# Two expert layers by seven products of quarters, with the layernorm split in two

## The chip, the cores and the metric

The kernel runs on one core of a Trainium2 chip. The metric is device time in microseconds for one execution, and each version is timed several times; the median is what counts. All data and all matmuls of the part in question are f32.

## The reference

A graph of 6250 nodes with 256 features each passes a graph convolution and then a mixture of experts. Cut to what matters:

```python
x = x + gnn(layernorm(x), edges)          # x@W, normalised neighbour sums, bias, PReLU
xf = layernorm(x)                          # (6250, 256)
# one routing decision for the whole batch, from the mean token: top 2 of 8 experts
h = gelu(einsum('nd,edf->enf', xf, W1) + b1)      # 256 -> 512, exact gelu
y = einsum('enf,efd->end', h, W2) + b2            # 512 -> 256
o = sum over the two experts of w[e] * y[e]
x = x + (layernorm(o + xf) * gamma + beta)
```

The mean token decides the two experts and their weights, so that every node goes through the same two experts. The change is only in `h`, `y` and the last layernorm.

## The kernel before, in words

The nodes lie in 49 tiles of 128 rows (the last has 106). The first 785 us or so are the graph convolution, the routing and the load of the two experts' weights. W2 and b2 are scaled by the experts' weights as they arrive (L1337), so that the two experts can be summed in one PSUM accumulation.

The expert stage (L1344 on) works on groups of four tiles, `TN = 4`: group 0 is one tile, groups 1 to 11 are whole, group 12 holds the short last tile. The order of every engine's work is the order in which it is written (`manual_schedule`), so each engine takes its instructions in line, and an instruction that waits holds all behind it on that engine. The steps of a group are:

- `take` (L998): SyncE loads the four tiles `xt` from HBM.
- `turn` (L1003): VectorE normalises each tile, `yt = (xt - mean) * rstd` (L1010); TensorE transposes it into PSUM (L1015); ScalarE copies the result to `xT` (L1017).
- `biases` (L1022, L1025): GpSimd adds b2 to `yt` and beta to `xt`, 1024 columns each.
- `layer_1` (L1362, L1366): for each expert and each of four blocks of 128 hidden units two matmuls of 512 columns (w1 stationary, xT moving), then a Gelu on ScalarE from PSUM to `hT`. It has three PSUM banks.
- `layer_2` (L1383 to L1402): for each tile eight matmuls of 256 columns (hT stationary, w2 moving) into one of three PSUM banks; then VectorE adds the result to `yt` (L1388), takes the statistics (L1389, L1390), adds epsilon (L1392); ScalarE takes the square root (L1393); VectorE finishes with a scalar_tensor_tensor (L1395), a reciprocal (L1398) and another scalar_tensor_tensor (L1399); SyncE stores the tile (L1402).

Gelu and Sqrt lie in different tables of ScalarE, so that each change from one to the other costs a table load, two per group. The loop over the groups looks ahead by `AH = 3`:

```python
        take(AH)
        layer_1(0)
        for i in range(len(groups)):
            if i + 1 < len(groups):
                layer_1(i + 1)
            if i + AH < len(groups):
                turn(i + AH, ps_x, nc.vector)
                biases(i + AH)
            if i + AH + 1 < len(groups):
                take(i + AH + 1)
            layer_2(i)
```

Of the kernel before, what the change touches and what calls it, by code (L numbers as in the profile page):

```python
# [12 lines left out]
F32 = mybir.dt.float32  # L13
# [5 lines left out]
AF = mybir.ActivationFunctionType  # L19
OP = mybir.AluOpType  # L20
# [5 lines left out]
P = 128  # L26
FAR = 16383
LN_EPS = 1e-5
TOP_K = 2
# [6 lines left out]
def gnn_moe_kernel(  # L36
# [34 lines left out]
    nc = tc.nc  # L71
    N, D = x.shape
    (E,) = src.shape
    NE, _, FF = w1.shape
    NT = -(-N // P)
    ND = D // P
    NF = FF // P
# [15 lines left out]
    whole = [(0, WE)] * WP  # L93
# [21 lines left out]
    def rows_of(i):  # L115
        return min(P, N - i * P)
# [6 lines left out]
    def bcast_row(pool, v, name, eng):  # L123
        t = pool.tile([P, v.shape[0]], F32, name=name)
        eng.dma_start(out=t, in_=v.partition_broadcast(P))
        return t
# [17 lines left out]
    rs = big.tile([P, NT], F32, name="rs")  # L144
    sc = big.tile([P, NT], F32, name="sc")
    bad_i = big.tile([P, 1], I32, name="bad_i")
    mean2 = big.tile([P, NT], F32, name="mean2")
    rstd2 = big.tile([P, NT], F32, name="rstd2")
# [50 lines left out]
    with ExitStack() as ph:  # L199
# [144 lines left out]
        for b in range(NSB):  # L344
            cmp_ = cmps[b % 2]
            nc.vector.tensor_scalar(cmp_, g_h, s_f[:, b : b + 1], None, op0=OP.is_gt)
            for w in range(NW):
                nc.tensor.matmul(
                    pcnt[:, w : w + 1], cmp_[:, w * P : (w + 1) * P], ones_b,
                    start=(b == 0 and w == 0), stop=(b == NSB - 1), skip_group_check=True,  # L350
# [12 lines left out]
        for b in (slice(0, NSB // 2), slice(NSB // 2, NSB)):  # L363
# [8 lines left out]
                op0=OP.mult, op1=OP.add,  # L372
            )
            nc.sync.dma_start(
                out=pk_at[:, b, :], in_=pk[:, b].rearrange("p b e f -> p b (e f)")
# [43 lines left out]
        st = ep.tile([P, NT, 6], F32, name="st")  # L419
# [11 lines left out]
        for w in range(NW):  # L431
            wins[w] = in_early(WE, I32)
            nc.gpsimd.indirect_dma_start(
                out=wins[w], out_offset=None, in_=dst.rearrange("(e o) -> e o", o=1),
# [128 lines left out]
        def of_window(w):  # L563
            return slice(w * WT, min((w + 1) * WT, NT))
# [15 lines left out]
        def root(w):  # L580
            nc.scalar.activation(dinv[:, of_window(w)], deg[:, of_window(w)], AF.Sqrt)
# [102 lines left out]
    with main:  # L684
# [241 lines left out]
        for n in range(1, NDT):  # L926
            for c in range(NHG):
                q = (n - G0) * NHG + c
# [41 lines left out]
    TN = 4  # L970
    AH = 3
    rest = NT % TN or TN
    groups = [(0, rest)] + [(t0, TN) for t0 in range(rest, NT, TN)]
    late = ctx.enter_context(tc.tile_pool(name="late", bufs=1))
    hp = ctx.enter_context(tc.tile_pool(name="hp", bufs=2))
    xp = ctx.enter_context(tc.tile_pool(name="xp", bufs=AH + 4))
    w1_sb = late.tile([P, TOP_K, ND, FF], F32, name="w1_sb")
    w2_sb = late.tile([P, TOP_K, NF, D], F32, name="w2_sb")
    b1_sb = late.tile([P, TOP_K, NF], F32, name="b1_sb")
    b2_sb = late.tile([P, D], F32, name="b2_sb")  # L980
    b2_t = late.tile([P, TOP_K, D], F32, name="b2_t")
    topw = late.tile([P, TOP_K], F32, name="topw")
    topi_i = late.tile([P, TOP_K], I32, name="topi_i")
    b1_r = late.tile([NE * NF, P], F32, name="b1_r")
    b1T = late.tile([P, NE * NF], F32, name="b1T")
    ahead = {}

    def take(i):

        yt = xp.tile([P, TN, D], F32, name="yt")  # L990
        xt = xp.tile([P, TN, D], F32, name="xt")
        xT = hp.tile([P, ND, TN * P], F32, name="xT2", bufs=AH + 2)
        ahead[i] = yt, xT, xt
        fill(i)

    def fill(i):
        t0, nt = groups[i]
        nc.sync.dma_start(  # L998
            out=ahead[i][2][:, :nt, :],
            in_=x1_d[t0 * P : (t0 + nt) * P, :].rearrange("(t p) d -> p t d", p=P),  # L1000
        )

    def turn(i, ps_x, eng):  # L1003

        t0, nt = groups[i]
        yt, xT, xt = ahead[i]
        px = ps_x.tile([P, ND, TN, P], F32, name="px")
        for t in range(nt):
            n = t0 + t
            eng.tensor_scalar(  # L1010
                yt[:, t, :], xt[:, t, :], mean2[:, n : n + 1], rstd2[:, n : n + 1],
                op0=OP.subtract, op1=OP.mult,
            )
            for k in range(ND):
                nc.tensor.transpose(px[:, k, t, :], yt[:, t, k * P : (k + 1) * P], ident)  # L1015
        for k in range(ND):
            nc.scalar.copy(xT[:, k, : nt * P], px[:, k, :nt, :].rearrange("p t e -> p (t e)"))  # L1017

    def biases(i):
        _, nt = groups[i]  # L1020
        yt, _, xt = ahead[i]
        nc.gpsimd.tensor_tensor(  # L1022
            yt[:, :nt, :], yt[:, :nt, :], b2_sb.unsqueeze(1).to_broadcast([P, nt, D]), OP.add
        )
        nc.gpsimd.tensor_tensor(  # L1025
            xt[:, :nt, :], xt[:, :nt, :], beta_bc.unsqueeze(1).to_broadcast([P, nt, D]), OP.add
        )

    with ExitStack() as ph:
        ph.enter_context(tc.manual_schedule(engines={PE, DVE, ACT, SP, POOL}))  # L1030
        ps_x = ph.enter_context(tc.tile_pool(name="ps_x", bufs=2, space=bass.MemoryType.PSUM))
        nc.scalar.dma_start(out=b1_r, in_=b1.rearrange("e (f p) -> (e f) p", p=P))
        gamma_bc = bcast_row(late, gamma, "gamma_bc", nc.scalar)
# [100 lines left out]
        def otherwise():  # L1134
            with tc.For_i(0, bad), ExitStack() as ph:  # L1135
# [163 lines left out]
                for i in range(AH):  # L1299
                    fill(i)  # L1300
                    if i < AH - 1:
                        turn(i, ps_x, nc.vector)
# [21 lines left out]
        with ExitStack() as once:  # L1324
            wp = once.enter_context(tc.tile_pool(name="wp", bufs=1))
            weights(lambda name: wp.tile([P, 1], F32, name=name))
            turn(AH - 1, ps_x, nc.gpsimd)
# [16 lines left out]
    with ExitStack() as ph:  # L1344
        ph.enter_context(tc.manual_schedule(engines={PE, DVE, ACT, SP, POOL}))
        op_ = ph.enter_context(tc.tile_pool(name="op", bufs=3))
        ps_x = ph.enter_context(tc.tile_pool(name="ps_y", bufs=1, space=bass.MemoryType.PSUM))
        ps_1 = ph.enter_context(tc.tile_pool(name="ps_1", bufs=3, space=bass.MemoryType.PSUM))
        ps_2 = ph.enter_context(tc.tile_pool(name="ps_2", bufs=3, space=bass.MemoryType.PSUM))

        hTs = {}

        def layer_1(i):
            t0, nt = groups[i]
            cols = min(nt * P, N - t0 * P)
            xT = ahead[i][1]
            hT = hTs[i] = hp.tile([P, TOP_K, NF, TN * P], F32, name="hT")
            for e in range(TOP_K):
                for f in range(NF):
                    p1 = ps_1.tile([P, TN * P], F32, name="p1")  # L1360
                    for k in range(ND):
                        nc.tensor.matmul(  # L1362
                            p1[:, :cols], w1_sb[:, e, k, f * P : (f + 1) * P],
                            xT[:, k, :cols], start=(k == 0), stop=(k == ND - 1),
                        )
                    nc.scalar.activation(  # L1366
                        hT[:, e, f, :cols], p1[:, :cols], AF.Gelu, bias=b1_sb[:, e, f : f + 1]
                    )

        def layer_2(i):  # L1370
            t0, nt = groups[i]
            yt, _, xt = ahead.pop(i)
            hT = hTs.pop(i)
            st = op_.tile([P, TN, 6], F32, name="st3")
            mv = op_.tile([P, TN, 2], F32, name="mv3")
            rs = op_.tile([P, TN], F32, name="rs3")
            for t in range(nt):
                n = t0 + t
                r = rows_of(n)
                p2 = ps_2.tile([P, D], F32, name="p2")  # L1380
                for e in range(TOP_K):
                    for f in range(NF):
                        nc.tensor.matmul(  # L1383
                            p2[:r], hT[:, e, f, t * P : t * P + r], w2_sb[:, e, f, :],
                            start=(e == 0 and f == 0), stop=(e == TOP_K - 1 and f == NF - 1),
                        )
                y = yt[:r, t, :]
                nc.vector.tensor_tensor(y, y, p2[:r], OP.add)  # L1388
                nc.vector.bn_stats(st[:r, t, :], y)  # L1389
                nc.vector.bn_aggr(mv[:r, t, :], st[:r, t, :])  # L1390
                rt = rs[:r, t : t + 1]
                nc.vector.tensor_scalar(rt, mv[:r, t, 1:2], LN_EPS, None, op0=OP.add)  # L1392
                nc.scalar.activation(rt, rt, AF.Sqrt)  # L1393

                nc.vector.scalar_tensor_tensor(  # L1395
                    y, y, mv[:r, t, 0:1], gamma_bc[:r], op0=OP.subtract, op1=OP.mult
                )
                nc.vector.reciprocal(rt, rt)  # L1398
                nc.vector.scalar_tensor_tensor(  # L1399
                    y, y, rt, xt[:r, t, :], op0=OP.mult, op1=OP.add  # L1400
                )
                nc.sync.dma_start(out=out[n * P : n * P + r, :], in_=y)  # L1402

        take(AH)
        layer_1(0)
        for i in range(len(groups)):
            if i + 1 < len(groups):
                layer_1(i + 1)
            if i + AH < len(groups):
                turn(i + AH, ps_x, nc.vector)  # L1410
                biases(i + AH)
            if i + AH + 1 < len(groups):
                take(i + AH + 1)
            layer_2(i)


# [31 lines left out]
```

## Time and profile before

| what | value |
|---|---|
| median of 3 runs | 1135.88 us (1135.06 to 1137.57) |
| the profiled execution, own time | 1139.88 us |
| its span | 1137.6 us |
| mean granted TensorE clock | 0.981 of full speed |
| TensorE busy over the span | 1090.0 us |
| VectorE busy | 709.5 us |
| ScalarE busy | 622.7 us |
| GpSimd busy | 539.6 us |

Busy times are those of one execution, taken by the hardware profiler. A row of the profile names a line of the kernel, the engine and operation, the output and inputs with their tile names, the shape, and the count; behind the bar stand the busy time in us, the mean duration of one in ns, and the idle time of the engine just before such instructions with what ended it. PE is TensorE's matmul, PEld its weight load, which runs beside matmuls; DVE is VectorE, ACT is ScalarE, POOL is GpSimd, SP is SyncE. One f32 matmul appears as two records, a transposition as one. Rows of the timeline begin with the start in us and the length of a run of like instructions.

### The profile page before, as it was taken

To read this page: it belongs to the slowest core of one execution; us is meant where nothing else is said; L and a number is where in the kernel's file an instruction comes from. 1 tells how busy PE (TensorE), PEld (TensorE's weight loads), DVE (VectorE), ACT (ScalarE), POOL (GpSimd) and SP (SyncE) were. 2 spreads that over 40 slices of the span, in tenths; PEclk is the share of its full clock that TensorE was granted. 3 is DMA by queue.
4 is the path that set the end of the run, shared out by engine and by line. 5 is a ranking of instruction groups with operands and counts; after the bars stand their busy time and mean duration, and the time that the engine had idled before them with its cause. 6 is when DMAs were issued, how large, how long until landed. Compare 5 with 4: busy or idle time off the path is not lost. (4 is left out here: it accounts for less than half of the span.)

```text
span 1137.6 us, 17950 instructions
## 1 busy us (share of the span) xinstructions
PE 1090.0 (96%) x6562; PEld 833.5 (73%) x6562; DVE 709.5 (62%) x1551; ACT 622.7 (55%) x1544; POOL 539.6 (47%) x473
## 2 busy tenths in 40 slices
PE   6888999999999999999999999887999999999997
PEld 5776788878887888788888888664566666666666
DVE  6778876777687877777777778744133333333335
ACT  3786577666667666667666667523533333333330
POOL 3701456777777676867666766524411111111000
PEclk9998999999999999999999999996999999999999
DMA  8749347676767677677777777533011111110001
GB/s 266 233 161 335 78 111 190 162 196 164 198 168 189 178 179 182 177 180 180 184 176 179 180 179 176 149 94 122 24 37 37 37 38 38 37 37 19 18 19 37
DMA packets 102750, 152.05 MB, mean 134 GB/s; under 512 B 10046, under 2 KB 48670, under 8 KB 102654
## 3 DMA queue, kind: packets, MB, share of 16 engines
q0 software_dynamic: 54080, 99.35, 34.8%
q1 hardware_dynamic: 45378, 48.93, 13.2%
q10 hardware_dynamic: 3196, 2.55, 0.8%
q8 instruction: 53, 0.87, 0.3%
q14 instruction: 43, 0.35, 0.1%
HBM read 123.42 MB, written 27.37 MB: 133 GB/s over the span
## 5 line engine op out<-in xcount | busy, mean ns | idle before, releaser
L830 POOL DMA_INDIRECT rows<-hl_d,g_src x360 | 410.8, 1141 | 189.2 <-PE pg L868 100.5
L737 PE MATMUL po<-hp,a_t 128*128 128x512 f32 x1911 | 480.6, 401 | 0.7 <-ACT a_t L721 0.7
L737 PEld LDWEIGHTS po<-hp,a_t 128*128 128x128 f32 x1911 | 350.6, 190 | 70.0 <-ACT a_t L721 1.1
L721 ACT CAST a_t<-pa 128x392 fp32r<-128x392 f32 x624 | 257.9, 502 | 212.1 <-PE pa L717 211.6
L476 DVE TENSOR_TENSOR unit<-iota,loT 128x2048 bf16<-128x2048 bf16 x156 | 190.4, 1221 | 45.2 <-PE pa L717 45.1
L1362 PE MATMUL p<-xT,w_sb 128*128 128x512 f32 (+2 forms) x416 | 174.0, 579 | 3.2 <-ACT xT L1017 2.1
L1383 PE MATMUL p<-w_sb,hT 128*128 128x256 f32 (+1 forms) x784 | 171.2, 379 | 0.0
L1383 PEld LDWEIGHTS p<-w_sb,hT 128*128 128x128 f32 (+1 forms) x784 | 147.9, 190 | 20.8 <-issue 0.9
L717 PEld LDWEIGHTS <-unit 128*128 128x128 bf16 x2496 | 121.6, 98 | 45.1 <-issue 24.3
L1388 DVE TENSOR_TENSOR yt<-yt,p 128x256 f32<-128x256 f32 (+1 forms) x49 | 20.6, 421 | 210.9 <-PE p L1383 210.9
L717 PE MATMUL pa<-unit 128*128 128x98 bf16 x2496 | 146.4, 210 | 5.0 <-DVE unit L476 2.5
L476 DVE TENSOR_TENSOR unit<-iota,keyT 128x1568 bf16<-128x1568 bf16 x156 | 150.8, 967 | 0.0
L1362 PEld LDWEIGHTS p<-xT,w_sb 128*128 128x128 f32 x416 | 80.1, 201 | 90.3 <-issue 82.9
L1022 POOL TENSOR_TENSOR yt<-yt,b_sb 128x1024 f32<-128x1024 f32 (+1 forms) x13 | 29.5, 2272 | 218.4 <-PE px L1015 206.3
L849 ACT ACTIVATE oh_g<-iota_f,g_dst 128x128 fp32r<-128x128 f32 x360 | 123.9, 423 | 0.0
L1366 ACT ACTIVATE hT<-p,b_sb 128x512 f32<-128x512 f32 (+2 forms) x104 | 67.4, 661 | 78.2 <-PE p L1362 78.1
L868 PE MATMUL pg<-rows,oh_g 128*128 128x512 f32 x360 | 106.1, 392 | 0.3 <-DMA rows<-hl_d,g_src 0.3
L1393 ACT ACTIVATE rs<-rs 128x1 f32<-128x1 f32 (+1 forms) x49 | 9.9, 203 | 150.0 <-DVE rs L1392 150.0
L868 PEld LDWEIGHTS pg<-rows,oh_g 128*128 128x128 f32 x360 | 68.1, 189 | 17.2 <-DMA rows<-hl_d,g_src 2.6
L851 ACT ACTIVATE oh_g<-oh_g 128x384 fp32r<-128x384 f32 (+1 forms) x140 | 67.2, 480 | 4.4
L772 DVE RECIPROCAL rstd<-rstd 128x1 f32<-128x1 f32 (+1 forms) x49 | 8.0, 164 | 87.5 <-ACT rstd L771 87.5
L404 PE MATMUL p<-w_sb,xT 128*128 128x256 f32 x196 | 47.4, 386 | 2.8 <-ACT xT L396 2.8
(192 smaller groups left out, 754.4 us busy)
## 6 DMA issues: line engine op xcount, KB each, us to landing
hl_d<-hp SPq DMA_DIRECT2D x7, 1792.0 KB
x_d<-x SPq DMA_DIRECT2D x49, 128.0 KB
xt<-x_d SPq DMA_DIRECT2D x12, 512.0 KB
out_dram<-yt SPq DMA_DIRECT2D x48, 128.0 KB
rows<-hl_d,g_src POOLq DMA_INDIRECT x360
xb<-in_x_dram SPq DMA_DIRECT2D x6, 896.0 KB
xs<-in_x_dram SPq DMA_DIRECT2D x39, 128.0 KB
xg<-in_x_dram SPq DMA_DIRECT2D x9, 128.0 KB
```

Source lines behind the costliest of these rows:

```text
L404: nc.tensor.matmul(p[:, t], xT[:, t, k, :], w_c[:, k, :], start=(k == 0), stop=(k == ND - 1),)
L476: nc.vector.tensor_tensor(oh, iota2[:, :m, :].unsqueeze(1).to_broadcast([P, HG // 2, m, 2]), v[:, s].rearrange("p (q t) -> p q t", t=2).un ...
L717: nc.tensor.matmul(pa[:, i].rearrange("p j h -> p (j h)"), oh_lo[:, q, :, t], oh_key[:, q, :, t], start=True, stop=True,)
L721: nc.scalar.copy(tiles[n][:, :, b * 2 * BG : (b + 1) * 2 * BG], pa.rearrange("p i j h -> p h (i j)"),)
L737: nc.tensor.matmul(pouts[n].rearrange("p k d -> p (k d)"), tiles[n][:, g, :], hp2[g // TB][:, g % TB].rearrange("p k d -> p (k d)"), start ...
L830: nc.gpsimd.indirect_dma_start(out=g_rows[j], out_offset=None, in_=hl_d, in_offset=bass.IndirectOffsetOnAxis(ap=g_src[:, j // GC, j % GC : ...
L849: nc.scalar.activation(oh[:, i, :], iota_f, AF.Abs, bias=g_neg[:, g, c : c + 1])
L851: nc.scalar.activation(oh, oh.bitcast(F32), AF.Relu, scale=-1.0, bias=1.0)
L868: nc.tensor.matmul(pouts[n].rearrange("p k d -> p (k d)"), oh[:, i, :], g_rows.pop(g * GC + c), start=False, stop=(c == GC - 1),)
L1362: nc.tensor.matmul(p1[:, :cols], w1_sb[:, e, k, f * P : (f + 1) * P], xT[:, k, :cols], start=(k == 0), stop=(k == ND - 1),)
L1366: nc.scalar.activation(hT[:, e, f, :cols], p1[:, :cols], AF.Gelu, bias=b1_sb[:, e, f : f + 1])
L1383: nc.tensor.matmul(p2[:r], hT[:, e, f, t * P : t * P + r], w2_sb[:, e, f, :], start=(e == 0 and f == 0), stop=(e == TOP_K - 1 and f == NF ...
```

## The change

Both layers of a whole group are computed by Winograd's form of Strassen's scheme: each of the two factors is cut into quarters, and seven products of quarters, or of sums and differences of quarters, take the place of eight. The sums of weights are formed once (`w2_t`, `w1_t`: eight VectorE operations of 1024 columns); those of the activations are formed for each group (`xs_` by four GpSimd subtractions, `h_s` by one GpSimd and three VectorE operations); and the products are put together by VectorE adds. Layer 2 is done so for groups 1 to 11, layer 1 for groups 2 to 11. The two pools of three PSUM banks become one of six. In layer 1 the two experts take turns, with three banks each.

The layernorm at the end of layer 2 is taken apart: the statistics stay in layer 2, one Sqrt and one Reciprocal for all four tiles (`root`) move to the middle of the next layer 1, and the last two scalar_tensor_tensor of each tile with its store (`ended`) move into the next group's layer 2, between its products. The normalisation of a coming group (`normed`) moves from `turn` to layer 2, one group earlier.

The core of the diff:

```diff
+        for k, p, q in (
+            (0, b12, b11), (1, b22, w2_t[:, 0]), (2, b22, b12), (3, b21, w2_t[:, 1]),
+        ):
+            nc.vector.tensor_tensor(w2_t[:, k], p, q, OP.subtract)
...
+            nc.vector.tensor_tensor(w1_t[:, k], p, q, op)
...
+        def combine_x(i):
...
+            for k, p, q in ((0, b12, b11), (1, b22, xs_[:, 0]), (2, b22, b12), (3, b21, xs_[:, 1])):
+                nc.gpsimd.tensor_tensor(xs_[:, k], p, q, OP.subtract)
+
+        def layer_1_whole(i, mid, three, tail):
...
+            def pr(e, n):
+                p = banks[e][{1: 0, 2: 2, 5: 1, 6: 0, 3: 2, 7: 0, 4: 0}[n]]
+                for f in range(HF):
+                    nc.tensor.matmul(
+                        p[:, f], w(e)[n - 1][:, f * P : (f + 1) * P], r[n - 1],
+                        start=n in (1, 2, 5, 3) and f == 0, stop=True, skip_group_check=True,
+                    )
+
+            def gelu(e, f0, c0, src=None):
+                for f in range(HF):
+                    at = hT[:, e, f0 + f, c0 : c0 + HC]
+                    nc.scalar.activation(
+                        at, at if src is None else src[:, f], AF.Gelu,
+                        bias=b1_sb[:, e, f0 + f : f0 + f + 1],
+                    )
+
+            def put(at, p, q):
+                nc.vector.tensor_tensor(at, p, q, OP.add)
...
+            pr(0, 1)
+            nc.scalar.copy(c11(0), X[0])
+            pr(0, 2)
+            put(c11(0), c11(0), Z[0])
+            three[0]()
+            pr(0, 5)
+            nc.scalar.copy(c22(0), Y[0])
+            pr(1, 1)
+            nc.scalar.copy(c11(1), X[1])
+            gelu(0, 0, 0)
+            pr(0, 6)
+            put(c12(0), c22(0), X[0])
+            pr(1, 2)
+            put(c11(1), c11(1), Z[1])
+            pr(0, 3)
+            pr(1, 5)
+            nc.scalar.copy(c22(1), Y[1])
+            gelu(1, 0, 0)
+            mid()
+            pr(0, 7)
+            put(c22(0), c22(0), X[0])
+            pr(1, 6)
+            put(c12(1), c22(1), X[1])
+            three[1]()
+            pr(1, 3)
+            put(c12(0), c12(0), Z[0])
+            gelu(0, HF, HC)
+            gelu(0, 0, HC)
+            pr(0, 4)
+            gelu(0, HF, 0, X[0])
+            pr(1, 7)
+            put(c22(1), c22(1), X[1])
+            put(c12(1), c12(1), Z[1])
+            three[2]()
+            gelu(1, HF, HC)
+            gelu(1, 0, HC)
+            tail()
+            pr(1, 4)
+            gelu(1, HF, 0, X[1])
...
+            def first():
+                step(2, a11, a21, OP.subtract, nc.gpsimd)
+                step(0, a21, a22, OP.add)
+
+            return (
+                first, lambda: step(1, h_s[:, 0], a11, OP.subtract),
+                lambda: step(3, a12, h_s[:, 1], OP.subtract),
+            )
...
+        def ended(i, t, mv, rs, yt, xt):
+            n = groups[i][0] + t
+            y = yt[:, t, :]
+            nc.vector.scalar_tensor_tensor(
+                y, y, mv[:, t, 0:1], gamma_bc, op0=OP.subtract, op1=OP.mult
+            )
+            nc.vector.scalar_tensor_tensor(
+                y, y, rs[:, t : t + 1], xt[:, t, :], op0=OP.mult, op1=OP.add
+            )
+            nc.sync.dma_start(out=out[n * P : (n + 1) * P, :], in_=y)
...
+            def product(p, a, b, start):
+                for t in range(HT):
+                    for e in range(TOP_K):
+                        for f in range(HF):
+                            nc.tensor.matmul(
+                                p[:, t], a[:, e, f, t * P : (t + 1) * P], b[:, e, f, :],
...
+            flush(roots)
+            product(pX, a11, b11, True)
+            if ends:
+                flush(ends, 1)
+            product(pY, h_s[:, 0], w2_t[:, 0], True)
+            add(y11, pX)
+            flush(ends, 1)
+            product(pX, h_s[:, 1], w2_t[:, 1], False)
+            add(y22, pY)
+            flush(ends, 1)
+            product(pZ, a12, b21, True)
+            add(y12, pX)
+            flush(ends, 1)
+            product(pX, h_s[:, 2], w2_t[:, 2], False)
+            add(y11, pZ)
+            flush(ends)
+            product(pY, h_s[:, 3], b22, False)
+            add(y22, pX)
+            if i + AH + 1 < len(groups):
+                normed(i + AH + 1)
+            product(pX, a22, w2_t[:, 3], False)
+            add(y12, pY)
+            for t in range(HT):
+                stats(t, yt, st, mv)
+            add(y21, pX)
+            for t in range(HT, TN):
+                stats(t, yt, st, mv)
+            nc.vector.tensor_scalar(rs, mv[:, :, 1], LN_EPS, None, op0=OP.add)
+
+            def root():
+                nc.scalar.activation(rs, rs, AF.Sqrt)
+                nc.vector.reciprocal(rs, rs)
...
         for i in range(len(groups)):
...
+            three = list(combine(i))
+
+            def tail():
+                if later is not None:
+                    if i == 0:
+                        normed(later)
+                    turn(later, ps_x, None)
+                    biases(later)
+                    combine_x(later)
+
+            def mid():
+                flush(roots)
+
+            if 2 <= i + 1 < len(groups) and whole(i + 1):
+                layer_1_whole(i + 1, mid, three, tail)
```

So product `(e, n)` of layer 1 is `pr(e, n)`: product n of expert e. `X`, `Y` and `Z` are the three banks of an expert, and `h_s[:, 3]`, the third VectorE combination of a group, stands in VectorE's line right behind the last `put`.

## The prediction

> **What bounds the kernel now.** I read the page's busy shares first, then the chain of waits, then a table of one group period, and last the rows of the operations that the change multiplies or removes.
>
> ```profile
> PE 1090.0 (96%) x6562; PEld 833.5 (73%) x6562; DVE 709.5 (62%) x1551; ACT 622.7 (55%) x1544; POOL 539.6 (47%) x473
> ```
>
> The 96% is a mean over two stages. The change touches only the expert stage, from about 785 us on, so the stage itself is read next (the chain: start, length, what).
>
> ```profile
> 862.87 13.73 PE p L1362 x32
> 876.60 0.87 PE px L1015 x8
> 877.47 13.81 PE p L1383 x64
> ```
>
> TensorE never waits here: layer 1 (L1362) takes 13.73 us, the transposes 0.87, layer 2 (L1383) 13.81; together 28.41 us a group. A table of one such period (columns: busy PE, PEld, DVE, ACT, POOL, then clock and DMA):
>
> ```profile
> 849.05:877.47 28.42, 28.42 (x105) 19.06 (x105) 9.83 (x32) 9.84 (x16) 4.66 (x2) 1.00 0.11 37
> ```
>
> VectorE and ScalarE are busy a third of it, at full clock, with the DMA engines at 0.11. So matmul time is the bound, and the other three engines have 18 us or more free per group, as a sum. Where their work stands in the order is another matter.
>
> ```profile
> L1383 PEld LDWEIGHTS p<-w_sb,hT 128*128 128x128 f32 x768 | 145.1, 190 | 20.1 <-issue 0.9
> L1366 ACT ACTIVATE hT<-p,b_sb 128x512 f32<-128x512 f32 x88 | 59.4, 686 | 68.5 <-PE p L1362 68.4
> L1393 ACT ACT_TABLE_LOAD x12 | 15.4, 1283 | 0.2
> L1399 DVE SCALAR_TENSOR_TENSOR yt<-yt,rs,xt 128x256 f32<-128x256 f32 x48 | 23.3, 484 | 2.6
> L1388 DVE TENSOR_TENSOR yt<-yt,p 128x256 f32<-128x256 f32 x48 | 20.2, 421 | 209.7 <-PE p L1383 209.7
> L1022 POOL TENSOR_TENSOR yt<-yt,b_sb 128x1024 f32<-128x1024 f32 x12 | 28.4, 2365 | 206.3 <-PE px L1015 206.3
> L1025 POOL TENSOR_TENSOR xt<-xt,beta_bc 128x256 f32<-128x256 f32 x1 | 1.2, 1177 | 0.0
> ```
>
> The reader should see how slow GpSimd is (2.37 us for 1024 columns, 1.18 for 256) and what one table load costs (1.28).
>
> **Matmuls removed and added.** One f32 matmul is two records. Layer 1 of a whole group is 16 matmuls of 512 columns = 32 records in 13.73 us, 429 ns a record, 858 a matmul. By sevens it is 7 products x 2 experts x 2 row halves = 28 matmuls of 256 columns. L1383 is that shape: 13.81/32 = 431.6 ns a matmul, so 28 make 12.08 us. Gain 1.65 us; ten groups (2 to 11): 16.5 us.
>
> Layer 2 is 32 matmuls of 256 columns; by sevens it is 7 x 2 tiles x 2 experts x 2 = 56 of 128 columns. The stage's rows of 128-column f32 matmuls are group 0's, at half clock:
>
> ```profile
> 778.87 2.63 PEld L1362 LDWEIGHTS p<-xT,w_sb 128*128 128x128 f32 x12 [2.55 <-ACT xT L1017]
> 778.87 4.24 PE L1362 MATMUL p<-xT,w_sb 128*128 128x128 f32 x16 [2.15 <-ACT xT L1017]
> ```
>
> At a granted clock of 0.50 twelve loads stand in 2.63 us, a record each 219 ns; at full clock half, 109 ns. The transposes, also 128 columns, run 8 in 0.87 us: 109 ns. So a matmul is 218 ns, 56 make 12.2 us, the gain is 1.6 us, eleven groups (1 to 11): 17.6 us. Bounds: were each load's 190 ns serial, layer 2 would take 56 x 0.38 = 21.3 us, a loss of 7.5 a group; the gain is gone at 13.81/56 = 247 ns. But half-clock loads of 201 ns mean (L1362) already keep a 219 ns cadence, with no 190 ns added to it, so I take 109 and keep 107 to 130 for the range. Sum of TensorE's gains: -34.1 us.
>
> **Work put beside it.** ScalarE per group: 8 gelus of 512 (5.5 us) become 16 of 256 (no row of that size; the rows of 512, 686 ns, and 128, 367, put one near 475, with up to 40 more for SBUF sources: 7.6) plus four copies of 512 (588 by L1017). With table loads and transposes' copies about 13 of 27. VectorE gains eight PSUM adds of 512 (by 421 ns for 256: 0.69 each), three SBUF combinations of 1024 (1.22 each) and seven adds instead of four, and loses 3 reciprocals and 3 offsets: about 18. GpSimd gains four 256-column subtractions (1.18 each) and a 1024 one (2.36): 4.7 becomes 11.8. None of the sums is the bound. SyncE issues the same four output DMAs a group, a group later, and the same load, ahead of them; nothing waits on that, as DMA is at 0.11. In layer 1 each expert has three PSUM banks, in layer 2 there are three for seven products; followed through the written order, only the two waits below come from their reuse.
>
> **Wait A: the square root is now queued inside layer 1.** `mid` puts Sqrt on ScalarE after a copy and two gelus of the second expert, with a table load on each side, and Reciprocal on VectorE ahead of the adds `put(c22(0))` and `put(c12(1))`. VectorE stands at Reciprocal until Sqrt is done, and the bank that product (0,4) writes waits for that put. From the end of product (1,5): semaphore and copy 0.6, second expert's two gelus 0.9, load 1.28, Sqrt 0.2, Reciprocal 0.16, put 0.69, about 3.9 us with semaphores. TensorE has (0,7), (1,6), (1,3) meanwhile, 6 matmuls x 0.43 = 2.6. So (0,4) comes 1.35 us late; the same queue makes (1,4) 0.37 late. Nine groups have both, 15.5, the last with 0.9 more on (1,4): +16.5 us. Before, the same two loads were hidden: three banks of layer 1 stood between ScalarE and TensorE, three of layer 2 between VectorE and TensorE, and no VectorE work fed a matmul of the same group.
>
> **Wait B: VectorE against GpSimd.** The trace shows what occurs when VectorE meets a running GpSimd op:
>
> ```profile
> 789.73 7.89 DVE L1010 TENSOR_SCALAR yt<-xt,mean,rstd 128x256 f32<-128x256 f32 x4
> 790.35 2.39 POOL L1022 TENSOR_TENSOR yt<-yt,b_sb 128x1024 f32<-128x1024 f32 x1
> 792.71 2.39 POOL L1025 TENSOR_TENSOR xt<-xt,beta_bc 128x1024 f32<-128x1024 f32 x1
> 978.78 1.38 DVE L1010 TENSOR_SCALAR yt<-xt,mean,rstd 128x256 f32<-128x256 f32 x4
> ```
>
> Four normalisations of 1.38 us take 7.89 when GpSimd is busy: each waits out one GpSimd op. Those have one SBUF input. The other way round, a GpSimd op beside a VectorE tensor_tensor with two SBUF inputs:
>
> ```profile
> 326.71 1.22 DVE L476 TENSOR_TENSOR unit<-iota,loT 128x2048 bf16<-128x2048 bf16 x1
> 326.82 1.92 POOL L830 DMA_INDIRECT rows<-hl_d,g_src  x1 [0.30 <-issue]
> ```
>
> That op takes 0.94 at its median and 1.92 here, so it was held until the VectorE op was over. No row shows a two-input f32 VectorE op started inside a GpSimd tensor_tensor. From below it costs nothing (its duration unchanged, as with PSUM inputs, 421 ns throughout); from above the whole rest of the GpSimd op. The Trainium skill ("SBUF — State Buffer", section "Who interferes with whom") says that a VectorE instruction with two SBUF inputs contends with a GpSimd instruction that reads SBUF, and that whoever came first keeps the port pair for its whole instruction. By the rows on two-input ops alone B could be 0; by the rule it is the full wait, and the normalisation rows behave as it says. I take the full wait.
>
> Its place: after layer 1 GpSimd starts b2 (2.36), beta (2.36) and four subtractions (4.7). In that stretch VectorE must run the third combination and, ahead of `add(y11, pX)`, both scalar_tensor_tensor of an old tile (`flush(ends, 1)`). Laying rows end to end: the combination waits 1.55 us for b2, the first STT 1.9 for beta, the second 0.6 for a subtraction. `add(y11)` is then late, and layer 2's third product, accumulating into the same bank, waits 2.75 us; the fifth 0.57. Groups 2 to 8, 7 x 3.32 = 23.2, and one more 2.15: +25.4 us. Groups 10 and 11 have no GpSimd biases any more. At the start `normed(3)` sits behind the eight weight combinations (1024 columns, two SBUF inputs), which alternate with GpSimd's biases: the transposes come 3.1 us late, others 1.1: +4.2 us.
>
> The end: layer 2 of group 12, unchanged, absorbs group 11's late `ended` (4 us of VectorE against 13.8 of matmuls), so the tail from the last matmul stays.
>
> **Sum.** -34.1 + 16.5 + 25.4 + 4.2 = +12.0 us. The profiled execution (span 1137.6, own time 1139.88, so 2.3 around it) would be 1151.9. It stands 4.0 above the median of the three runs, 1135.88, so the median goes to 1147.9.
>
> **Rivals.**
>
> 1. *The pair isn't locked against two-input f32 ops; faster.* Only A is left: -34.1 + 16.5 = -17.6, 1118.3. For: VectorE's 421 ns PSUM adds never stretch, and no row shows the case. Against: 7.89 for four, and 1.92 for 0.94. It decides at B below 1.5 us a group (17.6 - 4.2 over nine).
> 2. *128-column f32 matmuls are bound by their weight loads; slower still.* At 120 ns a record layer 2 gains 0.4 instead of 1.6; part of that fills stalls, so +8 beside the lock: 1156. At 130, +17: 1165. At 190, over 1200. For: PEld 190 ns per load against a 109 ns cadence. Against: the half-clock rows. It decides at 123 ns, where layer 2 gains nothing.
> 3. *Lock, but shorter waits.* GpSimd's 256-column ops at 0.95 instead of 1.18, or releases 0.2 us earlier, leave +5.6 to +7; a b2 or beta op 10% longer makes +17: 1141 to 1153.
>
> **How the numbers follow.** Lock as worked (1141 to 1156): 0.58. Load-bound, or stalls beyond these: 0.12. No lock: 0.24 (1116 to 1123). Half a lock, the waits eating the gain: 0.06, split over all three signs. A difference of 0.2% (2.3 us) is about the least that a measurement can tell. So faster 0.26, same 0.04, slower 0.70. As both signs hold much, the range runs from the no-lock case to 130 ns, 1117 to 1163; the likeliest case's own is 1141 to 1156.
>
> **What would show it.** Layer 2's records at 109 ns (else rival 2). TensorE idle of 1.3 us per group ahead of product (0,4), released by VectorE (A), and of some 2.7 ahead of layer 2's third product (B). VectorE combinations of 1024 lasting 2.5 us or more beside GpSimd ops, STTs of 2 us; if they stay at 1.22 and 0.48, rival 1 holds. Group period about 30.2 us; 26.9 without the lock. I am wrong if TensorE waits elsewhere: for hT from the gelus, for x loads, or for a bank at layer 1's start.

## The result, and the profile after

The changed kernel takes 1152.28 us (median of 4, 1150.51 to 1152.73) against 1136.72 of the kernel before (4 runs, 1135.06 to 1138.55): a ratio of 1.0134, 95% interval 1.0113 to 1.0154, so 15.6 us slower (13 to 17.5); 12 were forecast. The busy shares of the page after:

```profile
PE 1072.0 (93%) x7330; PEld 890.4 (77%) x7330; DVE 861.8 (75%) x1639; ACT 648.6 (56%) x1631; POOL 608.8 (53%) x524
```

TensorE is busy 18 us less and yet the kernel is slower, because TensorE waits now. The waits of TensorE in the expert stage (what waited, for what, us in total, times, longest):

```profile
PE p L1603 <- DVE yt L1611: 19.8, 8, 2.5
PE p L1417 <- DVE hT L1431: 11.7, 10, 1.2
```

L1603 are layer 2's products and L1611 is `add`; L1417 are layer 1's products and L1431 is `put`. Eight and nine groups (the last with two stops) are those of the forecast. One period in the chain of waits (start, length, what), where before stood three lines of TensorE alone:

```profile
892.43 6.92 PE p L1417 x32
...
900.77 1.28 ACT L1643
...
902.06 0.21 ACT rs L1643
...
902.39 1.27 DVE hT L1431 x2
...
904.72 1.88 DVE hT L1431 x3
906.59 2.93 DVE h_s L1513
909.52 2.50 DVE yt L1557
...
912.05 0.83 DVE yt L1560
912.88 0.34 DVE yt L1611
...
913.26 9.20 PE p L1603 x80
```

Read downwards, the chain goes from TensorE to ScalarE's table load and Sqrt, through VectorE's puts to the third combination (L1513) and the first scalar_tensor_tensor (L1557), and only then back to TensorE. That the puts stand behind the Reciprocal is seen in the timeline: VectorE is idle for 3.70 us at it, until the Sqrt is done, and the product behind the puts, (0,4), starts 1.19 us after TensorE has run dry.

```profile
902.30 0.18 DVE L1644 RECIPROCAL rs<-rs 128x4 f32<-128x4 f32 x1 [3.70 <-ACT rs L1643]
...
903.12 1.13 PE L1417 MATMUL p<-xs__11026,w_sb 128*128 128x256 f32 x4 [1.19 <-DVE hT L1431]
```

Why the third combination and the first scalar_tensor_tensor last 2.9 and 2.5 us is seen in the timeline of VectorE and GpSimd:

```profile
906.07 2.37 POOL L1035 TENSOR_TENSOR yt<-yt,b_sb 128x1024 f32<-128x1024 f32 x1 [14.78 <-PE px L1018]
906.51 3.01 DVE L1513 TENSOR_TENSOR h_s<-hT,h_s 128x1024 f32<-128x1024 f32 x1
908.40 3.33 POOL L1038 TENSOR_TENSOR xt<-xt,beta_bc 128x1024 f32<-128x1024 f32 x1
909.45 2.57 DVE L1557 SCALAR_TENSOR_TENSOR yt<-yt,mv,gamma_bc 128x256 f32<-128x256 f32 x1
911.69 0.91 POOL L1392 TENSOR_TENSOR xs__11396<-xT 128x256 f32<-128x256 f32 x1
```

They take turns. VectorE's 1.22 us of work ends 1.08 us after GpSimd's b2 addition ends; GpSimd's beta addition, 2.36 alone, then takes 3.33, as if it had been held until VectorE was done, 1.12 us after its start; the scalar_tensor_tensor, 0.48 alone, ends 0.29 after that. The same two rows as groups (mean ns in the next to last column), with a combination that meets no GpSimd work beside them:

```profile
L1557 DVE SCALAR_TENSOR_TENSOR yt<-yt,mv,gamma_bc 128x256 f32<-128x256 f32 x44 | 39.6, 901 | 0.0
L1513 DVE TENSOR_TENSOR h_s<-hT,h_s 128x1024 f32<-128x1024 f32 x11 | 29.7, 2704 | 0.0
L1513 DVE TENSOR_TENSOR h_s<-h_s,hT 128x1024 f32<-128x1024 f32 x11 | 13.4, 1219 | 0.0
```

Two f32 tensor_tensor of the same 1024 columns take 1.22 and 2.70 us, and the slow one is the one that meets GpSimd. That GpSimd is the cause is shown further on, where its additions are left out.

One thing was in no forecast. Five of the eight waits in layer 2 are followed by a stretch of slow matmuls. First two third products, each of 16 records, from the timeline; then windows on the two and on one of layer 1's stops (busy PE, PEld, DVE, ACT, POOL, granted clock, DMA):

```profile
913.26 2.05 PE L1603 MATMUL p<-w_t,h_s 128*128 128x128 f32 x16 [2.51 <-DVE yt L1611]
943.29 3.51 PE L1603 MATMUL p<-w_t,h_s 128*128 128x128 f32 x16 [2.51 <-DVE yt L1611]
```

```profile
913.20:915.30 2.10, 2.04 (x18) 2.04 (x19) 2.06 (x5) 0.00 (x0) 2.00 (x3) 1.00 0.22 70
943.20:946.90 3.70, 3.61 (x19) 3.61 (x20) 2.82 (x7) 0.00 (x0) 2.03 (x3) 0.57 0.21 71
903.00:904.20 1.20, 1.08 (x5) 0.98 (x6) 1.20 (x3) 1.19 (x3) 0.00 (x0) 1.00 0.00 0
```

The idle time is the same 2.51 us, but in one case the granted clock stays at 1.00 and in the other it is 0.57 over the window. The group periods show what it costs: counted from layer 1's first matmul, they are 31.67, 31.55, 30.03, 31.49, 30.04, 31.45, 30.05 and 31.24 us (the last with a wait 0.33 shorter). A slow stretch is worth about 1.5 us, and the five 7.6 us.

So the stretch from group 2's layer 1 to the last operation, 326.4 us before (806.02 to 1132.46) and 342.2 after (803.57 to 1145.75), is 15.7 us longer, and the parts add up like this:

| part | worked out from the profile after | us |
|---|---|---|
| layer 1 by sevens | 32 records in 6.92, so 56 in 12.11, not 13.73; ten groups | -16.2 |
| layer 2 by sevens | 112 records in 12.50, not 13.81; eleven groups | -14.4 |
| wait A | 30.03 - 12.11 - 0.87 - 12.50 = 4.55 a group for A and B with their restarts, of which A's part is 1.8 (0.17 of it lies at the transposes, see below); eight groups, and 2.65 in the last | +17.0 |
| wait B | 2.77 of the 4.55; eight groups, one 0.33 shorter | +21.8 |
| slow matmuls behind B | five | +7.6 |
| sum | measured: +15.7 | +15.8 |

### The profile page after: what moved, and what is told of

The parts are those of the page before. It is cut to its first block, busy times and chain, and to the rows that moved or that the text cites. A ratio compares the mean times of both kernels' runs of the same rounds, so it can differ in the third digit from the quotient of the medians.

```text
span 1150.9 us, 19776 instructions
## 1 busy us (share of the span) xinstructions
PE 1072.0 (93%) x7330; PEld 890.4 (77%) x7330; DVE 861.8 (75%) x1639; ACT 648.6 (56%) x1631; POOL 608.8 (53%) x524
## 5 line engine op out<-in xcount | busy, mean ns | idle before, releaser
L1603 PE MATMUL p<-w_t,h_s 128*128 128x128 f32 x528 | 71.7, 296 | 19.8 <-DVE yt L1611 19.8
L1603 PEld LDWEIGHTS p<-w_t,h_s 128*128 128x128 f32 x528 | 68.3, 210 | 21.3 <-DVE yt L1611 21.3
L1438 ACT COPY hT<-p 128x512 f32<-128x512 f32 x10 | 5.8, 583 | 123.0 <-PE p L1417 108.6
L1513 POOL TENSOR_TENSOR h_s<-hT 128x1024 f32<-128x1024 f32 x11 | 25.9, 2352 | 67.4 <-PE p L1603 67.4
L1425 ACT ACTIVATE hT<-hT,b_sb 128x256 f32<-128x256 f32 x120 | 53.2, 501 | 10.6 <-DVE hT L1431 10.5
L1611 DVE TENSOR_TENSOR yt<-yt,p 128x256 f32<-128x256 f32 x77 | 31.8, 413 | 34.7 <-PE p L1603 34.7
L1431 DVE TENSOR_TENSOR hT<-hT,p 128x512 f32<-128x512 f32 x80 | 51.6, 681 | 3.3 <-PE p L1417 3.0
```

What stands on the lines that cost most here:

```text
L1425: nc.scalar.activation(at, at if src is None else src[:, f], AF.Gelu, bias=b1_sb[:, e, f0 + f : f0 + f + 1],)
L1431: nc.vector.tensor_tensor(at, p, q, OP.add)
L1603: nc.tensor.matmul(p[:, t], a[:, e, f, t * P : (t + 1) * P], b[:, e, f, :], start=start and t + e + f == 0, stop=(e == TOP_K - 1 and f == ...
```

## The experiments

The theory is that A (Reciprocal waiting in VectorE's line) and B (VectorE locked out by GpSimd) are two separate waits that eat the gain. The chief rival is that VectorE simply has too much to do ahead of the adds. The runs were made on three chips: the first four on one, the next four on a second, the last on a third. On the second and third the kernel before takes 1163 and 1157 us; in the profiles from there the expert stage starts over 20 us later than in those of the first, so the difference lies in the graph part ahead of it. The ratios are against the kernel before on the same chip, and the periods compare directly.

**GpSimd's work later.**

```diff
                     turn(later, ps_x, None)
-                    biases(later)
-                    combine_x(later)
+                    behind.append(later)
...
             three[0]()
+            while behind:
+                biases(behind[0])
+                combine_x(behind.pop(0))
             pr(0, 5)
```

> GpSimd's two bias additions and four subtractions of a group are written one step later, behind its combination of h_s in the next layer 1, where VectorE mostly reads PSUM; VectorE's own order is untouched. Theory (the lock with GpSimd is what makes layer 2's third product wait): the third VectorE combination falls from 3.0 us to 1.22 and the first scalar_tensor_tensor from 2.6 to 0.48, the 2.7 us wait in layer 2 goes in all eight groups (22 us), and with it the stretches at about half clock behind it (7 us): 1152.3 - 29 = 1123 us. Rival (VectorE simply has too much work ahead of that add, with or without GpSimd): the wait shrinks by under 1 us a group, 1144 us or more. Second rival (the half clock is not caused by the wait): 1130 us.

Measured: 1160.89 us, ratio 1.0206 (1.0173 to 1.0240), worse than the change itself. Its timeline:

```profile
924.94 7.72 DVE L1027 TENSOR_SCALAR yt<-xt,mean,rstd 128x256 f32<-128x256 f32 x4
927.01 2.41 POOL L1035 TENSOR_TENSOR yt<-yt,b_sb 128x1024 f32<-128x1024 f32 x1
...
936.56 2.06 PE L1417 MATMUL p<-xT,w_t 128*128 128x256 f32 x4 [2.39 <-DVE hT L1431]
```

Wait B is gone from layer 2, as expected, but GpSimd's block now falls on the four normalisations of a coming group (`normed`). They take 7.72 us, where they take about 3.2 in the changed kernel and 1.38 undisturbed; all the adds and puts behind them on VectorE are late, and layer 1 stops for 0.59 and 2.39 us in eight groups. Three of the stops of 2.39 us have half clock behind them. It is the picture of the old profile's 7.89 us, which the prediction quotes and this expectation did not carry to the new place. The time lies in the rival's range, but the rival's reason does not hold, for layer 2 no longer waits and the third combination is back at 1.22 us. B needed another test.

**The Reciprocal later.**

```diff
                 nc.scalar.activation(rs, rs, AF.Sqrt)
-                nc.vector.reciprocal(rs, rs)
...
             put(c12(1), c12(1), Z[1])
+            flush(recips)
             three[2]()
```

> Only VectorE's Reciprocal is written later in layer 1, behind the last put; Sqrt and both table loads stay where they are on ScalarE. Theory (head of line: the puts stand behind a Reciprocal that waits for Sqrt): products (0,4) and (1,4) no longer wait, 1.8 us in nine groups and 2.6 in the last, 17 us: 1135 us, with the 2.7 us wait of layer 2 unchanged. Rival (ScalarE itself is late, because of table loads and more gelus): the wait moves to a copy or gelu and less than 5 us is won, 1147 us or more.

Measured: 1143.90 us, ratio 1.0065 (1.0043 to 1.0087). ScalarE's order is untouched, and yet A is gone from all groups but the last, which keeps a stop of 0.78 us. The wait that remains in the steady groups is B:

```profile
PE p L1605 <- DVE yt L1613: 21.0, 8, 2.7
```

So A came from the Reciprocal's place in the line, not from ScalarE's load. The move won 8 us and not 17, which fits neither number. The undisturbed period fell from 30.03 to 28.58, which is 1.45 of A's 1.8: B's idle rose by 0.15, from 2.51 to 2.66, and 0.17 was never A, since it stays about the transposes, which now stand between two products of layer 1. Six periods instead of five had slow matmuls (30.2 us). At the start the transposes of group 3 waited 2.42 us instead of 1.31, with half clock (0.54) behind them.

**Both later.**

```diff
+            while behind:
+                biases(behind[0])
+                combine_x(behind.pop(0))
...
+            flush(recips)
             three[2]()
```

> Both moves together. If the two waits are separate and the matmuls' gain is as the records show (1.62 us a layer 1, 1.31 a layer 2), the group period is 25.5 us, its matmuls alone, and the time is 1152.3 - 17 - 29 = 1106 us, 30 us under the kernel before. If each wait covered part of the other, 1112 to 1120. If another wait comes up behind them (gelus feeding layer 2, VectorE with 23 us of work in 25.5), above 1120.

Measured: 1153.28 us, ratio 1.0142 (1.0125 to 1.0159). The first edit's new wait rules here too; the normalisations last 1671 ns each on average. The stops of layer 1 are again 0.59 and 2.39 us, and seven of the eight long ones have half clock behind them. The time is above 1120, then, with another wait behind the two, but it is one that I had not named.

**The old group's pairs behind the adds.** The first two scalar_tensor_tensor pairs go behind the third add of layer 2, the rest behind the fifth.

```diff
             product(pX, a11, b11, True)
-            if ends:
-                flush(ends, 1)
             product(pY, h_s[:, 0], w2_t[:, 0], True)
             add(y11, pX)
-            flush(ends, 1)
...
             add(y12, pX)
-            flush(ends, 1)
+            flush(ends, 2)
...
             add(y22, pX)
+            flush(ends)
```

> GpSimd stays where it is; instead the scalar_tensor_tensor pairs of the old group (ended) are written behind the first three adds of layer 2. Theory: the third combination still lasts about 3.0 us beside GpSimd, and the first scalar_tensor_tensor may still be stretched, but the add that frees the bank stands ahead of it, so the third product waits 0.3 us or less and the half clock goes too: 1125 us (1122 to 1132). Rival (it is the third combination, not the scalar_tensor_tensor, whose delay counts): a wait of 1.5 us or more stays, 1137 us or more.

Measured: 1130.32 us, ratio 0.9940 (0.9924 to 0.9957): faster than both kernels, and in the range of the theory. The combination's row and the products' waits in this kernel:

```profile
L1513 DVE TENSOR_TENSOR h_s<-hT,h_s 128x1024 f32<-128x1024 f32 x11 | 29.7, 2701 | 0.0
```

```profile
PE p L1417 <- DVE hT L1431: 15.8, 17, 1.2
```

The combination is as slow as ever beside GpSimd, but layer 2 is missing from the list of waits. Here being locked out costs TensorE nothing in layer 2, because what frees a bank is no longer behind it. No period has slow matmuls: they went with the long wait. The seventeen stops include a new one of 0.6 us before (0,3), in seven groups, since the pairs now delay the puts.

**Pairs and Reciprocal together.** The moves of the pairs and of the Reciprocal in one kernel.

```diff
+            flush(ends, 2)
...
+            flush(recips)
             three[2]()
```

> The old group's scalar_tensor_tensor pairs behind the first three adds, and the Reciprocal behind the last put; GpSimd where the change has it. Theory (two separate queue waits): 1130.3 less the 17 us of the Reciprocal's wait, 1114 us; a wait of 0.6 us for a put in the next layer 1, which the later pairs brought, stays. Rival (the Reciprocal's wait is only moved on, as it seemed where it was moved alone and won 8 us and not 17): 1122 us or more.

Measured: 1141.74 against 1163.24 us on the second chip, ratio 0.9817 (0.9793 to 0.9841), 21.5 us less; 22.5 were expected. In the steady groups only the 0.6 us stops remain, seven in number, with one of 0.8 at the end, and the period is 26.51:

```profile
PE p L1417 <- DVE hT L1431: 5.0, 8, 0.8
```

**GpSimd and Reciprocal later, normalisations first.** As "both later", and:

```diff
-            add(y22, pX)
             if i + AH + 1 < len(groups):
                 normed(i + AH + 1)
+            add(y22, pX)
```

> Both moves of the third kernel, GpSimd's work behind its h_s combination and the Reciprocal behind the last put, and in addition the four normalisations of a coming group are written ahead of the add of layer 2's fifth product, that is before GpSimd starts. Theory (what made the first and third kernels slow was those four, each waiting for one of GpSimd's additions): they take 1.4 us instead of 7.7, no product waits in the steady groups, the period is 25.5 to 25.9 us and the time 1108 us (1105 to 1114). Rival (GpSimd's block of 10 us meets another two-input operation that counts, such as the first combination of h_s): 1120 us or more.

Measured: 1139.00 against 1163.24 us, ratio 0.9793 (0.9769 to 0.9817), 24.2 us less where 28.5 were expected (22.5 to 31.5 by the range). One add moved behind the normalisations turns the ratio of 1.0142 into 0.9793:

```profile
906.77 1.38 DVE L1027 TENSOR_SCALAR yt<-xt,mean,rstd 128x256 f32<-128x256 f32 x4
...
908.32 2.36 POOL L1517 TENSOR_TENSOR h_s<-hT 128x1024 f32<-128x1024 f32 x1 [14.93 <-PE p L1608]
```

```profile
885.95:911.59 25.64, 25.64 (x178) 24.00 (x177) 20.37 (x41) 12.53 (x25) 10.63 (x8) 1.00 0.13 43
```

The normalisations end before GpSimd begins, in a gap in which VectorE had waited for the fifth product anyway. The second fence is a window over one period: TensorE is busy 25.64 of 25.64 us at full clock, against 28.41 before; that is the 25.48 of its matmuls (12.11, 0.87 and 12.50) and 0.16 about the transposes. What is missing to 28.5 lies at the start. GpSimd's combination of h_s, which in the change came later, now runs beside the sums of weights, so that a further sum takes 2.71 us; the transposes of group 3 behind them wait 4.76 us, and layer 2 of group 0 after that takes 4.79 us instead of 3.62.

**GpSimd's bias additions left out.** Nothing is moved.

```diff
-    def biases(i):
+    def biases(i, late=False):
+        if late:
+            return
...
-                    biases(later)
+                    biases(later, late=True)
```

> The changed kernel with the two GpSimd bias additions of groups 3 to 12 left out (their output lacks b2 and beta), nothing else moved. Theory (GpSimd's long additions hold VectorE's combination and its first scalar_tensor_tensor): the combination falls to 1.3 to 2.0 us, the scalar_tensor_tensor to about 0.5 to 1.3, the 2.7 us wait of layer 2 goes, and with it the half clock: 1152.3 - 29 = 1123 us, 1120 to 1127. Rival (VectorE's own work makes the wait): 1140 us or more.

Measured: 1149.84 against 1163.24 us, ratio 0.9884 (0.9851 to 0.9916), 13.4 us less than the kernel before, where 1123 against 1136.5 had been expected. VectorE's order and work are those of the change, and:

```profile
L1515 DVE TENSOR_TENSOR h_s<-hT,h_s 128x1024 f32<-128x1024 f32 x11 | 13.4, 1219 | 0.0
L1559 DVE SCALAR_TENSOR_TENSOR yt<-yt,mv,gamma_bc 128x256 f32<-128x256 f32 x44 | 24.7, 562 | 0.0
```

The combination is back at 1.22 us and layer 2 waits nowhere. The period is 27.25 us, which is 25.48 of matmuls and 1.77 for A and the transposes. The rival of too much VectorE work falls.

**Normalisation first at the start.** As the kernel with GpSimd and Reciprocal later and the normalisations first, with `normed(AH)` written ahead of the eight sums of weights.

```diff
+        take(AH)
+        normed(AH)
         for k, p, q in (
             (0, b12, b11), (1, b22, w2_t[:, 0]), (2, b22, b12), (3, b21, w2_t[:, 1]),
```

> As the kernel with GpSimd later and the normalisations first, and in addition the normalisation of group 3 at the start is written ahead of the eight sums of weights. Theory: the transposes of group 3 no longer wait at the start (4 us where GpSimd's work was moved): 4 us below that kernel. Rival: VectorE waits for the load of group 3's tiles ahead of the sums, so that layer 1 of group 2 starts late: the same or 1 to 4 us above it.

Measured: 1143.37 against 1163.24 us, ratio 0.9823 (0.9791 to 0.9856): 4 us above that kernel (the two intervals overlap), the rival's number but not its wait for a load:

```profile
816.88 7.89 DVE L1027 TENSOR_SCALAR yt<-xt,mean,rstd 128x256 f32<-128x256 f32 x4
...
837.07 1.10 PE L1419 MATMUL p<-xs__10659,w_t 128*128 128x256 f32 x4 [3.14 <-DVE w_t L1384]
...
842.84 0.20 ACT L1538 ACTIVATE rs<-rs 128x1 f32<-128x1 f32 x1 [11.68 <-DVE rs L1537]
843.62 2.05 PE L1419 MATMUL p<-xs__10659,w_t 128*128 128x256 f32 x4 [4.58 <-issue]
```

The transposes no longer wait, but the four normalisations met GpSimd's start biases at once, and the sums behind them were late for layer 1. A second stop, of 4.58 us, has no releaser in the profile. By the written order it is the same lateness: the layernorm of group 0 stands behind the sums on VectorE, ScalarE stood 11.68 us at its Sqrt, and the copy that empties the bank of product (0,6) came behind that Sqrt.

**The start freed of GpSimd.** As the kernel with normalisations first, with the additions of groups 1 and 2 moved behind the subtractions for group 3; in every later group, too, GpSimd now subtracts before it adds.

```diff
-        for i in range(AH):
-            biases(i)
+        biases(0)
...
+            for v in behind:
+                combine_x(v)
+            if i == 2:
+                biases(1)
+                biases(2)
+            while behind:
+                biases(behind.pop(0))
```

> As the kernel with GpSimd later and the normalisations first; in addition the GpSimd bias additions of groups 1 and 2 leave the start and follow the subtractions for group 3 in layer 1 of group 2. Theory (at the start too it is GpSimd's long additions that stretch VectorE's eight sums of weights from 0.7 to 2.8 us and so delay group 3's normalisation): the sums end 10 us earlier, the transposes' wait of 4.8 us and the half clock behind it (1.2 us) go, 5 to 6 us below that kernel's ratio of 0.979, so 0.974 to 0.976 of the kernel before on the same chip. Rival: the third combination of layer 1 of group 2 now meets the moved additions and its layer 2 waits for 2 us or more: 0.977 or above.

Measured: 1134.30 against 1157.35 us, ratio 0.9773 (0.9739 to 0.9808), which is not clear of 0.9793 (the intervals overlap) and lies in the rival's range. The timeline shows the sums unlocked, and the next instruction that is held, in the layernorm of group 0:

```profile
810.59 0.69 DVE L1371 TENSOR_TENSOR w_t<-w_sb,w_t 128x512 f32<-128x512 f32 x1
...
829.07 2.32 DVE L1545 SCALAR_TENSOR_TENSOR yt<-yt,rs,xt 128x256 f32<-128x256 f32 x1
```

The start to group 2's layer 1 is 6.2 us shorter in the profiles (24.4 for 30.65), but layer 1 of group 2 now stops for 0.7, 1.4 and 0.7 us, so that nearly half of it is given back. The rival had put this wait in layer 2, which waits nowhere.

## Why the prediction was right, and where its sum was off

The sign, the two waits, their places and the group counts held, and the undisturbed period came to 30.03 us for 30.2. The total came to +15.6 us for +12. But four terms were off, and they partly cancelled.

- *Layer 1's gain*: 16.5 forecast, 16.2 measured. A 256-column matmul is 432 ns, as taken.
- *Layer 2's gain*: 17.6 forecast, 14.4 measured. What was off is the cadence of 109 ns, taken from transposes and half-clock rows; the records run at 12.50/112 = 111.6. Over 112 records 2.6 ns make 0.29 us a group, about a fifth of the gain. Rival 2 (load-bound at 120 and more) did not come.
- *Wait A*: 16.5 forecast, 17.0 measured, of which 1.4 lies at the transposes (0.17 in each of eight groups) and was in no term; (0,4) was 1.36 late for 1.35. The Reciprocal's move shows the mechanism.
- *Wait B*: 25.4 forecast, 21.8 measured. The third product's wait of 2.75 came as 2.67, but the fifth's 0.57 never came: the four subtractions take 0.73 us alone, not the 1.18 of the one row that I priced them by. That row ran beside VectorE's scaling of w2 and may itself have been held (argued, not shown). For the lock, the rule of the Trainium skill ("SBUF — State Buffer", section "Who interferes with whom"), on which the full wait was taken, is what the trace shows: with GpSimd's additions gone, 2.70 us fell to 1.22. Rival 1 would have shown 1.22 with them.
- *The start*: 4.2 forecast; the transposes of group 3 waited 1.3. The sums of weights are of 512 columns each (128x512 in the trace), not of 1024 as the texts ahead of the result say. Four of the eight sums of weights, each beside a GpSimd addition, took 2.7 to 2.9 us, one 1.1, and three, after the last addition, 0.69; I had all eight alternate.
- *Slow matmuls behind a wait*: not in the sum, +7.6. The sum took a wait to cost its length and no more; that is the term it left out. Five of the eight waits in layer 2 had half clock behind them, none of the ten of 1.2 us or less. The Trainium skill ("TensorE: Matmul & The Clock Gate", section "Why this matters for your kernels") asks for no gaps over about 3 us between bursts of matmuls. By it waits of 2.7 us would be safe and a stop of 3.14 us would not; here the first were not, one of 2.17 us of idle among them, and the 3.14 us of "normalisation first at the start" had full clock behind it. The measurement decides. What picks the cases stays open: the length of the stop alone does not.

Against the forecast, the slow matmuls and layer 2's smaller gain cost 7.6 and 3.2 us more, B and the start 3.6 and 2.9 less. That the total came within 4 us owes something to luck: the mechanism was right, but errors of 10.8 and 6.5 us met from opposite sides.

It was not tried which of GpSimd's two operands makes the lock, nor whether VectorE's operations of one SBUF input other than these normalisations fall under it.

## What to carry to other kernels

Before a change puts VectorE work with two SBUF inputs, or f32 normalisations, beside GpSimd work, write the two engines' timelines over each other and ask which VectorE instruction that frees a bank stands behind one that can be locked out. Then move that instruction forward, or move GpSimd's work to where VectorE reads PSUM, and look there for the next instruction that would be held before running: the same move was worth +1.4% and -2.1% depending on one line. A periodic stop of TensorE can also cost more than its length: here removing the stop of 2.5 us won 22 us, and removing that of 1.2 us won 8.

## What the runs showed of the hardware that was not expected

- Idle stretches of TensorE of 2.2 to 2.5 us were followed by about half the granted clock in five of eight cases of the changed kernel, for some 1.5 us of extra time each. With 2.4 us it was three and seven of eight in the two kernels with GpSimd's work later, with 2.3 to 2.7 six of eight in that with the Reciprocal later; with 1.2 us or less none of ten.
- VectorE and GpSimd took turns one by one when both had work in line: four weight sums of 0.69 us took 2.8 us each beside GpSimd additions of 2.36, which took 2.8 as well.
- GpSimd subtracts 256 f32 columns in 0.73 us and adds 1024 in 2.36.
